# One ring for all row tiles, six tables with interleaved halves, new step times, and the reciprocal deviation by logarithm and exponential, in a two-layer graph kernel

## The chip, the cores and the metric

The kernel runs on one core of one Trainium2 chip. The metric is the device time of one execution in microseconds, the median of several runs. Engines are named as in the profile: PE (TensorE, matrix products), DVE (VectorE), ACT (ScalarE), POOL (GpSimd) and SP (SyncE, which here only issues transfers).

## What is computed

For each of 32 batches, x has 512 channels (C) and 1024 positions (N), in f32. The reference, cut to what matters:

```
h = relu(layernorm(x))                       # over the 1024 positions
q, k = wq . h, wk . h                        # one number per position
att = softmax(leaky(q[None, :] + k[:, None]))# 1024 x 1024, slope 0.01
x = x + relu(wm @ (h @ att.T) + bm)          # wm is the adjacency, 512 x 512
h = relu(layernorm(x))
x = x + W.T @ h + bias                       # W = adjacency * adjacency, by elements
```

The layer norm divides by sqrt(variance + 1e-5). The scores depend on a sum of two numbers only. So the kernel doesn't form the 1024 x 1024 matrix: it sorts the positions by q, makes running sums of the value rows in sorted order, weighted by exp(q) and exp(0.01 q), and picks for each position the two sums at the point where its own k changes the sign.

## The kernel before, in words

One batch goes through these steps. The names are functions of the kernel, the line numbers those of the profile.

- *load* (L400): four row tiles of 128 x 1024 f32 (512 KB) by SP's queue. *stats* (L414, L415, DVE): mean and variance. *norm* (L419, ACT): the square root of variance + eps. *slopes* (L423, L425, DVE): its reciprocal, and minus the mean times it. *relu* (L433, ACT): scales, shifts and clips the tile, in place in the first layer.
- *scores* (L445 PE, L450 ACT, L451): q and k as products; ACT copies them to SBUF, and a DMA writes them to a small DRAM row. *row* (L456) reads it back as a broadcast to 128 partitions, *columns* (L461, L466) turns it to columns.
- *rank* (L487, L492, L496, DVE): counts for each position how many q are smaller. *lower* (L503, ACT) counts by signs for k. *factors* (L473 to L480), *to_rows* (L523 to L529) and *from_rows* (L533 to L543) work out row numbers from the counts: `idx` for the scatter, `idg` for the gather.
- *value* (L550, PE, 64 products per batch) makes the value rows, *spread* (L557, ACT) copies them to SBUF, *scatter* (L562, L563, POOL, eight indirect DMAs) writes them in sorted order to a table `td` in DRAM, along with q as the last column. A row has 513 floats.
- *fetch* (L580, SP) reads the sorted rows back (2.36 MB) once all eight scatters have landed. *weights* (L587 to L592, ACT) and *later* (L600, L604, DVE) make the exponentials, *stationary* (L623, POOL) triangular masks times them, *totals* (L612, L613, L617) the sums of weights.
- *scan* (L636, L639, PE) makes running sums in nine steps. After each step, *sums* copies the last row into the next block of values as a carry (L648, L649, ACT), copies the sums to one of two tiles `t` (L651, L652, ACT), and SP writes those to the table (L654, L655). A next step waits for the carry.
- *gather* (L660, POOL, eight indirect DMAs) reads for each position one triple row: both sums and the value row between them. *excess*, *divide* (L669 to L681), *weigh* (L685, ACT) and *combine* (L689, DVE) put them together.
- *turn* (L696, PE transposes; L698, DVE) adds the result to x, which *reload* (L406, SP) has read anew. Then *stats*, *norm*, *slopes* and *relu* of the second layer follow, *lift* (L439, DVE) adds the bias, *propagate* (L703, PE, 64 products) and *finish* (L711, DVE) end the batch, and SP writes the tile out (L715).

Each table holds 1152 (9 x 128) triples of rows, two halves of 9 x 64. In a triple (k = 0, 1, 2) the first two places are the sums, which the scan writes, and the third is the value row that the scatter writes. In the table of before, the first half of the triples (o = 0) comes first and the second half (o = 1) after it; the scan's sums stand only in the first half. Five tables are used in turn (`TABLES`). The pads (L362 to L367) are rows that no position fills.

The work of all 32 batches is one list that is sorted by time (L719 to L769): a step of batch b stands at `b * T + PLAN[step]`, T is 80.647, with a shift for each of the first batches (FIRST, 5 batches) and of the last ones (LAST). These times only set an order: each engine executes its instructions in it, one after another, and each queue issues so too. Semaphores then see to dependences. The order is not altered by anything else (`manual_schedule`).

SBUF holds seven row tiles in a pool `xp`, seven in `yp` and four in `hp`. A new tile takes the oldest slot of its pool and waits until its last reader is done.

Of the kernel before, what the change touches and what calls it, by code (L numbers as in the profile page):

```python
# [9 lines left out]
F32 = mybir.dt.float32  # L10
BF16 = mybir.dt.bfloat16
U32 = mybir.dt.uint32
AF = mybir.ActivationFunctionType
ALU = mybir.AluOpType
# [11 lines left out]
TABLES = 5  # L26
PLAN = {
    "adjacency": (-108.2,),
    "biases": (103.637,),
    "columns": (-0.644,),  # L30
    "combine": (
        295.175, 296.981, 297.681, 298.56, 293.456, 294.898, 296.312, 299.441, 298.758,
        299.991, 297.356, 298.478, 299.289, 299.451, 296.18, 297.782,
    ),
    "compare_mask": (-39.924,),
    "divide": (279.776,),
    "excess": (274.084,),
    "factors": (31.052,),
    "fetch": (71.51,),
    "finish": (356.071, 361.635, 372.571, 377.123, 391.802, 417.732, 398.837, 420.531),  # L40
    "from_rows": (87.236,),
    "gather": (260.35, 264.453, 263.071, 264.447, 267.501, 263.458, 263.983, 262.344),
    "later": (82.669,),
    "lift": (343.707, 352.288, 361.264, 350.629),
    "load0": (-132.547,),
    "load1": (-83.561,),
    "load2": (-110.642,),
    "load3": (-58.45,),
    "lower": (25.135, 20.956, 15.44, 19.087, 14.733, 13.756, 46.166, 37.237),
    "masks": (-18.987,),  # L50
    "norm0": (-31.509,),
    "norm1": (326.35,),
    "pads": (-73.925,),
    "propagate": (346.423, 349.207, 352.169, 365.765, 371.233, 382.761, 381.981, 389.706),
    "rank": (17.984, 18.872, 20.129, 19.992, 25.594, 25.16, 26.367, 26.318),
    "reload0": (283.236,),
    "reload1": (289.947,),
    "reload2": (275.592,),
    "reload3": (294.126,),
    "relu0": (-21.389, -21.25, -20.652, -20.617),  # L60
    "relu1": (336.308, 336.463, 336.836, 338.53),
    "row": (1.149,),
    "scan": (88.672, 94.082, 102.974, 119.344, 135.342, 151.67, 171.394, 183.726, 197.836),
    "scatter": (49.236, 49.927, 49.759, 49.383, 53.226, 50.436, 50.301, 52.611),
    "scores": (-2.312,),
    "slopes0": (-23.106,),
    "slopes1": (327.104,),
    "spread": (10.418, 15.798, 4.081, 13.981, 26.765, 25.953, 18.654, 18.733),
    "square": (58.25,),
    "stationary": (82.87, 113.617, 158.362),  # L70
    "stats0": (-66.042, -57.278, -62.987, -37.25),
    "stats1": (317.836, 318.803, 321.449, 320.562),
    "sums": (90.354, 96.928, 115.433, 127.043, 139.894, 157.148, 175.982, 190.223, 211.407),
    "to_rows": (21.507, 28.041),
    "totals": (87.7,),
    "turn0": (305.575, 305.673, 305.631, 305.894),
    "turn1": (311.888, 311.406, 311.889, 311.693),
    "turn_adjacency": (-56.308,),
    "value": (4.654, 14.383, -2.141, 4.319, 19.868, 19.769, 15.801, 17.456),
    "weigh": (288.834, 288.645, 287.955, 288.582, 291.515, 291.657, 292.795, 290.433),  # L80
    "weights": (79.137,),
}
FIRST = {
    "columns": ((-42.337, 0), (-5.231, 0), (-2.394, 0), (1.4, 0), (-0.267, 0)),
    "combine": (
        (1.654, -0.5293), (1.005, -0.3379), (12.151, -0.5389), (4.662, 1.8664), (-2.717, -0.8902),
    ),
    "divide": ((-6.522, 0), (2.121, 0), (-5.673, 0), (4.125, 0), (-1.132, 0)),
    "excess": ((-1.018, 0), (2.997, 0), (-2.579, 0), (2.459, 0), (2.332, 0)),
    "factors": ((12.008, 0), (36.085, 0), (20.556, 0), (-17.001, 0), (38.59, 0)),  # L90
    "fetch": ((-13.827, 0), (-9.161, 0), (-4.562, 0), (-10.853, 0), (-1.955, 0)),
    "finish": (
        (-7.71, -0.5057), (2.749, -0.1853), (2.024, 0.1345), (-9.528, -0.7581), (-1.467, 0.1212),
    ),
    "from_rows": ((-16.545, 0), (143.901, 0), (-18.52, 0), (2.567, 0), (44.362, 0)),
    "gather": (
        (-9.577, -0.9485), (-11.32, -0.6577), (-4.449, 0.1722), (-9.629, -0.1251), (0.796, 0.0714),
    ),
    "later": ((-7.518, 0), (-7.347, 0), (-5.042, 0), (-3.972, 0), (4.883, 0)),
    "lift": (  # L100
        (18.493, -0.0414), (7.449, -0.8273), (15.021, 1.1896), (12.507, -0.3341), (13.391, 1.5716),
    ),
    "load0": ((-55.083, 0), (-28.454, 0), (-82.787, 0), (-89.755, 0), (-8.172, 0)),
    "load1": ((-101.05, 0), (-75.105, 0), (-63.613, 0), (-51.655, 0), (-0.85, 0)),
    "load2": ((-75.638, 0), (-49.315, 0), (-74.213, 0), (-72.717, 0), (-4.898, 0)),
    "load3": ((-124.613, 0), (-99.018, 0), (-53.784, 0), (-32.124, 0), (2.903, 0)),
    "lower": (
        (-42.973, -0.9302), (-15.708, -0.6946), (-9.312, -0.2971), (10.582, -0.0696), (34.856, -0.2988),
    ),
    "norm0": ((-83.601, 0), (-72.105, 0), (-7.68, 0), (-14.053, 0), (-0.379, 0)),  # L110
    "norm1": ((7.168, 0), (3.555, 0), (4, 0), (0.017, 0), (-5.5, 0)),
    "propagate": (
        (2.872, -0.6898), (4.018, -0.2375), (-1.06, -0.345), (-1.214, -0.2813), (-1.309, -0.0657),
    ),
    "rank": (
        (-28.589, 0.7379), (-2.87, -0.0721), (-9.055, 1.3394), (2.403, 0.1874), (-13.459, 0.0458),
    ),
    "reload0": ((-6.546, 0), (6.572, 0), (3.271, 0), (5.826, 0), (-6.189, 0)),
    "reload1": ((-1.43, 0), (8.813, 0), (6.594, 0), (3.913, 0), (-1.301, 0)),
    "reload2": ((-12.374, 0), (4.019, 0), (-0.514, 0), (8.006, 0), (-11.757, 0)),  # L120
    "reload3": ((1.756, 0), (10.208, 0), (8.663, 0), (2.721, 0), (1.743, 0)),
    "relu0": (
        (-45.821, -0.4234), (-30.012, 0.2683), (5.354, 1.299), (-1.745, 0.0153), (3.565, -0.5324),
    ),
    "relu1": (
        (9.188, 0.8499), (2.193, -0.013), (10.49, -0.8921), (-4.148, -0.0533), (5.006, -0.1977),
    ),
    "row": ((-24.758, 0), (-11.86, 0), (-11.402, 0), (-3.047, 0), (-12.236, 0)),
    "scan": (
        (-10.549, -0.0092), (-6.067, 0.0274), (-9.758, -0.1074), (-3.442, 0.0619), (-0.102, -0.002),  # L130
    ),
    "scatter": (
        (-17.315, 0.2618), (-11.153, 0.1679), (0.523, -0.1955), (-0.018, 0.156), (10.696, 0.3981),
    ),
    "scores": ((-62.327, 0), (-16.533, 0), (-8.214, 0), (-8.615, 0), (-9.042, 0)),
    "slopes0": ((-60.963, 0), (-35.582, 0), (0.527, 0), (-21.398, 0), (0.491, 0)),
    "slopes1": ((7.724, 0), (5.221, 0), (19.376, 0), (1.394, 0), (7.329, 0)),
    "spread": (
        (-20.028, 0.1376), (-6.015, 0.992), (8.718, 0.232), (10.947, -0.0528), (-1.297, 0.1468),
    ),  # L140
    "stationary": (
        (-9.533, -0.0517), (-0.489, 0.0893), (-5.756, -0.1735), (-6.449, -0.1248), (4.497, -0.0251),
    ),
    "stats0": (
        (-104.674, 0.702), (-77.356, 0.023), (-31.203, 0.8527), (-27.97, 0.4148), (-4.885, 0.5116),
    ),
    "stats1": (
        (1.142, 1.1308), (0.139, -0.1099), (5.326, 1.0258), (1.699, -0.7252), (-0.894, -0.2163),
    ),
    "sums": (  # L150
        (-8.312, -0.031), (-5.309, 0.0498), (-7.225, -0.0992), (-0.666, 0.0426), (1.428, -0.0107),
    ),
    "to_rows": (
        (-22.19, 0.5865), (-4.005, -0.1384), (-1.537, -0.1666), (6.658, -0.9288), (6.396, -0.6681),
    ),
    "totals": ((-8.637, 0), (-5.524, 0), (-8.905, 0), (-5.244, 0), (1.382, 0)),
    "turn0": ((-0.966, 0.9178), (2.05, 1.1944), (5.507, -0.2416), (13.541, 1.3559), (6.422, 0.711)),
    "turn1": (
        (-5.235, 2.5311), (3.046, 0.3048), (6.19, 0.6659), (-2.074, -0.6081), (-2.371, 1.8837),
    ),  # L160
    "value": (
        (-38.477, -0.2052), (-18.574, 0.6364), (-1.298, 0.5607), (-3.097, 0.6813), (-5.339, -0.0078),
    ),
    "weigh": (
        (-11.307, 0.6182), (-3.966, -0.0933), (3.637, 0.3643), (2.741, 0.6417), (-2.168, 0.2103),
    ),
    "weights": ((-7.839, 0), (-5.68, 0), (-3.274, 0), (-1.31, 0), (1.823, 0)),
}
LAST = {
    "columns": ((7.408, 0), (2.218, 0), (11.624, 0), (6.617, 0), (9.298, 0)),  # L170
    "combine": (
        (184.23, -0.647), (7.018, -0.6426), (4.54, 0.7582), (4.732, 1.7176), (6.572, -0.8403),
    ),
    "divide": ((175.719, 0), (2.439, 0), (-3.673, 0), (2.742, 0), (4.328, 0)),
    "excess": ((172.709, 0), (3.234, 0), (1.536, 0), (-5.245, 0), (8.713, 0)),
    "factors": ((-5.036, 0), (-12.606, 0), (17.188, 0), (-12.641, 0), (7.562, 0)),
    "fetch": ((5.667, 0), (1.995, 0), (5.156, 0), (-1.217, 0), (1.341, 0)),
    "finish": (
        (752.974, -0.831), (173.796, 0.1634), (35.432, 0.5906), (9.597, -0.1536), (9.066, 0.2434),
    ),  # L180
# [616 lines left out]
```

## Time and profile before

| | us |
|---|---|
| runs | 2375.03, 2374.95, 2371.89 (median 2374.95) |
| profiled execution, span | 2372.9 |
| PE busy | 2295.2 |
| DVE busy | 1952.6 |
| ACT busy | 1599.8 |
| POOL busy | 720.7 |

The profile's span runs from the first instruction to the last of the one profiled execution, for which no other time is given; two of the three runs are about 2 us over the span, one is 1 us below it. Lines of the profile name a kernel line, an engine and the tile that is written and read (`vs<-td` is the fetch, `td<-t` a write of sums, `g<-td,idg` a gather). A group shows its busy time, the mean of one instruction, and the idle time of the engine ahead of it with what ended that. In the page, DMA queue q1 holds the transfers that SP issues, q0 POOL's, q10 ACT's; the share is that of all 16 DMA engines of the core over the span. A window gives for a stretch of the span the busy time of each engine, the clock that was granted to PE, the DMA engines' share and the rate. The chain of waits follows the work back from what ended last, at each step to what released it. The names turn[0], totals[2] and the like mean a step of that batch.

### The profile page before, as it was taken

Reading aid. Unit: us, or ns where it says so; the run is one execution under the profiler, and the core shown is the slowest. Engines: PE = TensorE matmul, PEld = TensorE weight load, DVE = VectorE, ACT = ScalarE, POOL = GpSimd, SP = SyncE. Lnnn points to the kernel's source line nnn. Section 1 sums busy time; section 2 is a strip of 40 time slices with the busy share of each in tenths; the row PEclk is TensorE's granted clock in tenths of the full one; section 3 lists DMA queues with packets and bytes.
Section 4 is the critical chain, followed back from the end, with each engine's and each line's share of the span. In section 5 each row is a group of like instructions: output and inputs, shape, how many; then the busy total and the mean of one; then the engine's idle time right before and its main releaser. Section 6 shows DMA issues by size and latency. Waiting matters only on the chain.

```text
span 2372.9 us, 28069 instructions
## 1 busy us (share of the span) xinstructions
PE 2295.2 (97%) x7568; PEld 1011.5 (43%) x7568; DVE 1952.6 (82%) x5008; ACT 1599.8 (67%) x2880; POOL 720.7 (30%) x973
## 2 busy tenths in 40 slices
PE   7787999999999999999999999999999999999997
PEld 3233444444444444444444444444444444443443
DVE  7457888888888888888888888888888888888875
ACT  4576776766777766777676777676677676677551
POOL 2233333233333233233223233323333323233310
PEclk9988999999999999999999999999999999999998
DMA  6678888989999998999999999899988898998972
GB/s 222 171 181 277 284 284 277 296 269 276 287 290 285 296 286 266 277 299 283 288 292 266 276 294 287 287 291 272 268 291 276 288 302 253 276 282 269 311 294 79
DMA packets 206894, 643.45 MB, mean 271 GB/s; under 512 B 29120, under 2 KB 29248, under 8 KB 206736
## 3 DMA queue, kind: packets, MB, share of 16 engines
q1 hardware_dynamic: 142944, 355.74, 53.9%
q0 software_dynamic: 57344, 268.99, 30.7%
q10 hardware_dynamic: 6448, 16.92, 2.3%
q8 instruction: 61, 1.00, 0.2%
q14 instruction: 97, 0.79, 0.1%
HBM read 429.94 MB, written 211.60 MB: 270 GB/s over the span
## 4 chain that ended last, share of the span: by engine, by line
PE 85%; DMA 5%; DVE 5%; ACT 2%; issue 1%; POOL 1%; SPq 0%; ACTq 0%; another core or an unknown queue 0%; POOLq 0%; DVEq 0%
PE pg L703 34%; PE pv L550 33%; PE sc L639 10%; PE tr L696 4%; DMA vs<-td 2%; PE pq L445 2%; PE sc L636 1%; DVE g L689 1%; DVE st L414 1%; DMA g<-td,idg 1%; DMA td<-v,idx 1%; DVE junk L492 1%; ACT x L433 0%; DVE junk L487 0%; DMA x<-in_x_dram 0%
## 5 line engine op out<-in xcount | busy, mean ns | idle before, releaser
L703 PE MATMUL pg<-h,wsq 128*128 128x512 f32 x2048 | 911.2, 598 | 12.8 <-ACT h L433 12.8
L550 PE MATMUL pv<-wmT,x 128*128 128x512 f32 x2048 | 908.8, 598 | 5.9 <-ACT x L433 4.4
L703 PEld LDWEIGHTS pg<-h,wsq 128*128 128x128 f32 x2048 | 382.8, 191 | 517.4 <-issue 476.1
L550 PEld LDWEIGHTS pv<-wmT,x 128*128 128x128 f32 x2048 | 382.0, 191 | 499.1 <-issue 452.6
L623 POOL TENSOR_TENSOR sm<-mask_a,wc 128x192 f32<-128x192 f32 x96 | 51.9, 540 | 1254.9 <-DVE wc L600 785.7
L689 DVE SCALAR_TENSOR_TENSOR g<-g,cf 128x512 f32<-128x512 f32 x512 | 357.9, 756 | 46.4 <-ACT g L685 44.3
L648 ACT COPY vs<-sc 1x512 f32<-1x512 f32 x256 | 145.3, 567 | 272.9 <-PE sc L639 208.6
L563 POOL DMA_INDIRECT td<-v,idx x256 | 272.4, 1064 | 149.3 <-POOL v L562 36.3
L639 PE MATMUL sc<-vs,sm 128*64 128x512 f32 x1024 | 282.6, 621 | 21.3 <-POOL sm L623 11.1
L503 ACT ACTIVATE junk<-qrow,qk 128x1024 bf16<-128x1024 f32 x256 | 294.0, 1148 | 5.5 <-DMA qrow<-qd 2.5
L660 POOL DMA_INDIRECT g<-td,idg x256 | 243.5, 951 | 147.4 <-issue 71.5
L698 DVE SCALAR_TENSOR_TENSOR y<-tr,nbm,y 128x512 f32<-128x512 f32 x256 | 174.4, 744 | 66.3 <-PE tr L696 61.2
L711 DVE SCALAR_TENSOR_TENSOR y<-pg,bm_sb,y 128x512 f32<-128x512 f32 x256 | 185.8, 731 | 32.4 <-PE pg L703 32.0
L651 ACT COPY t<-sc 128x512 f32<-128x512 f32 x288 | 168.0, 583 | 40.7 <-DMA td<-t 35.3
L433 ACT ACTIVATE x<-x,nmr,rstd 128x1024 f32<-128x1024 f32 x128 | 148.6, 1231 | 64.9 <-DVE nmr L425 64.9
L492 DVE TENSOR_SCALAR_CACHE_REDUCE junk<-qrow,qk,cnt 128x896 bf16<-128x896 f32 (+6 forms) x224 | 180.5, 806 | 8.2
L685 ACT ACTIVATE g<-g,cf 128x512 f32<-128x512 f32 x256 | 167.7, 712 | 6.4 <-DVE cf L679 5.3
L487 DVE TENSOR_SCALAR_CACHE_REDUCE junk<-qrow,qk 128x128 bf16<-128x128 f32 (+6 forms) x224 | 166.0, 741 | 6.6
L414 DVE BATCH_NORM_STATS2 st<-x 128x6 f32<-128x512 f32 x256 | 162.7, 677 | 9.6 <-DMA x<-in_x_dram 9.6
L439 DVE TENSOR_TENSOR y<-y,bias_sb 128x1024 f32<-128x1024 f32 x128 | 154.3, 1219 | 16.0 <-ACT h L433 16.0
L557 ACT COPY v<-pv 128x512 f32<-128x512 f32 x256 | 141.8, 579 | 29.7 <-PE pv L550 14.0
L414 DVE BATCH_NORM_STATS2 st<-y 128x6 f32<-128x512 f32 x256 | 160.4, 668 | 0.0
(111 smaller groups left out, 1923.1 us busy)
## 6 DMA issues: line engine op xcount, KB each, us to landing
vs<-td SPq DMA_DIRECT2D x192, 384.8 KB
td<-t SPq DMA_DIRECT2D x576, 128.2 KB
x<-in_x_dram SPq DMA_DIRECT2D x128, 512.0 KB
y<-in_x_dram SPq DMA_DIRECT2D x128, 512.0 KB
out_dram<-y SPq DMA_DIRECT2D x128, 512.0 KB
qrow<-qd ACTq DMA_DIRECT2D x32, 512.0 KB
td<-v,idx POOLq DMA_INDIRECT x256, 8.3
g<-td,idg POOLq DMA_INDIRECT x256, 13.8
```

The costliest lines, as they stand in the source:

```text
L414: nc.vector.bn_stats(st[:, i, :], s.x[c][:, ts(i, HALF)])
L492: nc.vector.tensor_scalar(junk[:, j * P :], s.qrow[:, j * P :], qc, first, ALU.is_lt, ALU.add, accum_out=s.cnt[:, 1, j : j + 1],)
L503: nc.scalar.activation(junk, s.qrow, AF.Sign, bias=s.qk[:, 1, j : j + 1], accum_out=s.sgn[:, j : j + 1])
L550: nc.tensor.matmul(pv, s.h[c][:, ts(j, P)], wmT[:, c, :], start=(c == 0), stop=(c == NC - 1))
L563: i = nc.gpsimd.indirect_dma_start(tds[s.b % TABLES][:, :], bass.IndirectOffsetOnAxis(ap=s.idx[j // 4][:, j % 4 : j % 4 + 1], axis=0), v[: ...
L639: nc.tensor.matmul(p[ts(k, HP), :], m[:, k, :], s.vs[h][:, 0:C], start=True, stop=True)
L651: nc.scalar.copy(t[:, 0:C], p)
L660: nc.gpsimd.indirect_dma_start(s.g[:, j, :], None, tds[s.b % TABLES][0 : 3 * NB * HP, :].rearrange("(s k) w -> s (k w)", k=3), bass.Indire ...
L689: nc.vector.scalar_tensor_tensor(r, s.g[:, j, k * W : k * W + C], s.cf[:, k, j : j + 1], r, ALU.mult, ALU.add)
L698: nc.vector.scalar_tensor_tensor(xh, pt, nbm[:, o : o + 1], xh, ALU.max, ALU.add)
L703: nc.tensor.matmul(pg, wsq[:, r, ts(c, P)], s.h[r][:, ts(i, HALF)], start=(r == 0), stop=(r == NC - 1),)
L711: nc.vector.scalar_tensor_tensor(xh, s.pg.pop((c, i)), bm_sb[:, c : c + 1], xh, ALU.add, ALU.add)
```

## The change

1. *One ring.* The pools `xp`, `yp` and `hp` become one pool of 18 tiles.
2. *New times.* PLAN, FIRST and LAST have new numbers, with six batches in FIRST and LAST; T stays. *pads* and *holes* have a time per table.
3. *Tables.* Six in place of five, and four DRAM rows for q and k in place of two. The halves of a table are interleaved in blocks of 64, so that the sorted rows lie on 128 partitions in one transfer: three fetch DMAs per batch in place of six. Row numbers are worked out to match, with one small DVE operation more. A gather's source is now the whole table.
4. *Pads.* A pad tile per table, with its own memsets; three DMAs per table.
5. *Holes.* The places k = 0, 1 of the second halves are written by no step. A new step fills them once per table, with the first 9 x 64 x 1026 numbers of x (2.36 MB), by one DMA of SP's queue from DRAM to DRAM.
6. *Reciprocal deviation.* ACT makes exp(-0.5 ln(variance + eps)) and DVE improves it by one Newton step. The set of ACT tables is loaded once ahead of all.

The diff, without the numbers of the plan. `-`/`+` lines stand in the order of the code.

```diff
-TABLES = 5
+TABLES = 6
+ROWS = 18
+QROWS = 4
 PLAN = {
-    "adjacency": (-108.2,),
+    "adjacency": (-1664.69,),
...
-    "pads": (-73.925,),
+    "holes": (-0.276, 48.82, 31.32, 105.504, 154.636, 169.546),
+    "pads": (-50.462, -29.172, -74.596, -76.152, -71.484, -110.523),
...
-    xp = ctx.enter_context(tc.tile_pool(name="xp", bufs=7))
-    yp = ctx.enter_context(tc.tile_pool(name="yp", bufs=7))
-    hp = ctx.enter_context(tc.tile_pool(name="hp", bufs=NC))
+    xp = ctx.enter_context(tc.tile_pool(name="xp", bufs=ROWS))
...
-        rows = td.rearrange("(o h s k) w -> o s h k w", o=2, s=HP, k=3)
-        return rows[:, :, h : h + n, 2, :]
+        rows = td.rearrange("(h p k) w -> p h k w", p=P, k=3)
+        return rows[:, h : h + n, 2, :]
...
-    root = const.tile([P, 1], F32, name="root")
-    nc.scalar.activation(root, eps_sb, AF.Sqrt)
+    nc.scalar.preload_act_table_set("natural_log_exp_and_others")
...
-    def pads(s):
-        pad = vp.tile([P, W], F32, tag="v", name="pad")
+    def pads(s, i):
+        pad = vp.tile([P, W], F32, tag="v", name=f"pad_{i}")
         nc.vector.memset(pad, 0.0)
         nc.vector.memset(pad[:, C : C + 1], FAR)
-        for td in tds:
-            for o in range(2):
-                nc.sync.dma_start(sorted_rows(td, 0, NB - 1)[o, 0], pad[0 : NB - 1, :])
-                nc.sync.dma_start(sorted_rows(td, NB - 1, 1)[o, :, 0], pad[0:HP, :])
+        for o in range(2):
+            nc.sync.dma_start(sorted_rows(tds[i], 0, NB - 1)[o * HP], pad[0 : NB - 1, :])
+        nc.sync.dma_start(sorted_rows(tds[i], NB - 1, 1)[:, 0], pad)
+
+    def holes(s, i):
+        rows = tds[i].rearrange("(h o s k) w -> h o s (k w)", o=2, s=HP, k=3)[:, 1, :, 0 : 2 * W]
+        flat = x.rearrange("b c n -> (b c n)")[0 : NB * HP * 2 * W]
+        nc.sync.dma_start(rows, flat.rearrange("(h s w) -> h s w", h=NB, s=HP))
...
     def norm(s, layer):
         s.std = sp.tile([P, NC], F32, tag=f"std{layer}", name=f"std{layer}_{s.b}")
-        nc.scalar.activation(s.std, s.mv[:, :, 1], AF.Sqrt, bias=eps_sb)
+        nc.scalar.activation(s.std, s.mv[:, :, 1], AF.Ln, bias=eps_sb)
+        s.rstd = sp.tile([P, NC], F32, tag=f"rstd{layer}", name=f"rstd{layer}_{s.b}")
+        nc.scalar.activation(s.rstd, s.std, AF.Exp, scale=-0.5)
 
     def slopes(s, layer):
-        s.rstd = sp.tile([P, NC], F32, tag=f"rstd{layer}", name=f"rstd{layer}_{s.b}")
-        nc.vector.reciprocal(s.rstd, s.std)
+        t = sp.tile([P, NC], F32, tag=f"step{layer}", name=f"step{layer}_{s.b}")
+        nc.vector.scalar_tensor_tensor(t, s.mv[:, :, 1], EPS, s.rstd, ALU.add, ALU.mult)
+        nc.vector.scalar_tensor_tensor(t, t, -0.5, s.rstd, ALU.mult, ALU.mult)
+        nc.vector.scalar_tensor_tensor(s.rstd, t, 1.5, s.rstd, ALU.add, ALU.mult)
...
-        odd = 3.0 * NB * HP
+        odd = 3.0 * HP
...
-        nc.vector.scalar_tensor_tensor(s.idx[i], block, 3.0, rk, ALU.mult, ALU.add)
+        nc.vector.scalar_tensor_tensor(
+            s.idx[i], block, 3.0 * (P - PAIRS), rk, ALU.mult, ALU.add
+        )
...
-        nc.vector.scalar_tensor_tensor(s.idg, pair, 1.0, block, ALU.add, ALU.add)
+        nc.vector.tensor_scalar(block, block, float(P - PAIRS), 1.0, ALU.mult, ALU.add)
+        nc.vector.tensor_tensor(s.idg, pair, block, ALU.add)
...
-            for o in range(2):
-                d = nc.sync.dma_start(t[ts(o, HP)], sorted_rows(tds[s.b % TABLES], 3 * i, 3)[o])
-                for k in s.sc:
-                    tc.add_manual_dep(d.ins, k.name, DONE, reason="any of them may hold a row")
+            d = nc.sync.dma_start(t, sorted_rows(tds[s.b % TABLES], 3 * i, 3))
+            for k in s.sc:
+                tc.add_manual_dep(d.ins, k.name, DONE, reason="any of them may hold a row")
...
-        nc.sync.dma_start(td[ts(ha, HP), 0, :], t[0:HP, :])
-        nc.sync.dma_start(td[ts(hb, HP), 1, :], t[HP:P, :])
+        nc.sync.dma_start(td[ts(2 * ha, HP), 0, :], t[0:HP, :])
+        nc.sync.dma_start(td[ts(2 * hb, HP), 1, :], t[HP:P, :])
...
-            tds[s.b % TABLES][0 : 3 * NB * HP, :].rearrange("(s k) w -> s (k w)", k=3),
+            tds[s.b % TABLES].rearrange("(s k) w -> s (k w)", k=3),
```

The instructions that the change puts in another order in the ramp, as the compiled order has them: SP issues the adjacency first of all, then eleven row tiles; the pads of tables 0 and 1 come after their memsets, which stand on DVE between the rank pieces of batch 0; then the holes of table 0; after fetch[0] the holes of tables 2 and 1, and later, between the writes of sums of batches 0 and 1, those of tables 3, 4 and 5.

## The prediction

> **What bounds the kernel now.** I read the busy times and the DMA queues of the page first, then the windows by stage, then what TensorE (PE) waited for, then the chain of waits of the first 240 us.
>
> ```profile
> PE 2295.2 (97%) x7568; PEld 1011.5 (43%) x7568; DVE 1952.6 (82%) x5008; ACT 1599.8 (67%) x2880; POOL 720.7 (30%) x973
> ...
> q1 hardware_dynamic: 142944, 355.74, 53.9%
> q0 software_dynamic: 57344, 268.99, 30.7%
> ```
>
> ```profile
> 0.00:240.00 240.00, 187.36 (x628) 77.85 (x628) 143.45 (x454) 146.82 (x278) 66.88 (x107) 0.93 0.74 211
> 240.00:2100.00 1860.00, 1859.18 (x6195) 823.57 (x6196) 1606.51 (x4126) 1324.69 (x2379) 594.89 (x789) 1.00 0.91 284
> 2100.00:2373.00 273.00, 248.62 (x746) 110.08 (x744) 202.62 (x430) 128.30 (x225) 58.92 (x77) 0.95 0.72 238
> ```
>
> The columns of the windows are length, PE, PEld, DVE, ACT, POOL, granted clock, DMA share, GB/s. From 240 to 2100 us PE is busy for 1859.18 of 1860 us: that stage is PE's own work, which the change leaves alone. Idle are 52.6 us in the first 240 us (the ramp) and 24.4 in the last 273 (the tail). Only there can the change gain, though it can lose anywhere. The ramp's idle time is made by transfers:
>
> ```profile
> 67.55 0.06 ACT w L589
> ...
> 68.94 0.57 POOL sm L623
> 69.52 0.04 issue
> 69.56 1.72 PE sc L639 x4
> ...
> 96.79 7.00 DMA td<-v,idx
> 103.93 0.62 SPq L580
> ...
> 107.26 9.96 DMA vs<-td
> ...
> 118.01 0.52 POOL sm L623
> ...
> 146.16 6.35 DMA td<-t
> ...
> 171.35 1.01 POOL g L660
> ...
> 180.13 16.16 DMA g<-td,idg
> ```
>
> This is the chain (start, length, what). Batch 1's scatter lands at 103.8, its sorted rows are fetched from 103.93 to 117.3, and only then come its masks (118.01) and totals. Batch 0's gathers start at 171.35 and end at 196.3; the first transposes of batch 0 (turn[0], L696) start at 214.15. PE executes in a written order, so what comes late here is late at the end, unless other work stands in front of it.
>
> **Removed: table loads.** ACT has 61+28+27+6+1 = 123 table loads of 1.283 us, 157.8 us; one stays. In the steady stage ACT is busy for 1324.7 of 1860 us and PE waits for nothing, so they are worth 0. In the ramp there are 8, one of them on the chain (93.64, ahead of the scatter): at most -1.3, and nothing if something later holds that scatter.
>
> **Added: Exp and Newton step.** Per normalisation one more ACT activation (about 0.30, as L419) and three DVE operations of 0.16 in place of a reciprocal of 0.17: +0.6 us of latency. 64 of them give 19 us of ACT and 20 us of DVE (82% to 83%), hidden under PE. Only the first and the last are on the path: +0.6 each.
>
> **Fetch and tables.** Three fetch DMAs of 128 partitions instead of six of 64 save SP three issues of 0.61, at most -1.8 per batch. The bytes stay (2.36 MB), so between -1.8 and 0; I take 0. A sixth table frees nothing that is waited for in the steady stage.
>
> **One ring.** 7+7+4 slots become 18. In both orders a slot is asked for after its last reader, with some PE work in between in every case, so I cost it at 0. The cover is PE's queue of work in order; if it were gone, each late tile would cost about one landing, 4 to 6 us (x from 166.18 took 4.20, the first one 5.74).
>
> **New times.** In PE's written order, counted with the durations of the rows, the work ahead of totals[0] to [2] grows by 6.7, 2.2 and 1.5 us, that ahead of turn[0] shrinks by 1.1. So alone they move the ramp by about -1 to +2. In the tail the last chain (ACT h before the last pg, 10.3 us of wait) gets 0.6 longer and up to 5 us more work is laid beside it: -2 to +1, I take 0.
>
> **Added: holes.** Six DMAs from DRAM to DRAM on SP's queue copy 2.36 MB each, 14.2 MB in the ramp. By the compiled order scatter[b] waits for holes[b], and the gathers too. No row of before is such a copy. Bounds for one: 6.4 us, if all 16 engines work at q0's rate (268.99 MB in 30.7% of 16 x 2372.9 us = 23.1 GB/s per engine); 15.7 us, if it gets no more than q1's mean over the span (355.74 MB / 2372.9 us = 150 GB/s). Added bytes on the queue gain nothing. The nearest row has the same bytes on the same queue: the fetch, 103.93 to 117.31, 13.4 us from issue to landing; less some 2 us for three issues, I take **11.4 us**, 13.4 to landing.
>
> The same table holds the case for and against. At 240 us x 0.26 = 62 us the engines are free long enough for six holes of 6.4 to 8.5 us (8.5 is q1's 17.4 GB/s per engine on all 16), but not where they stand.
> - fetch[0]: the holes of table 0 are queued in SP behind pads that need a DVE memset, and that memset stands behind four rank pieces (1.7 + 3 x 2.05 us), the maximum (1.8) and another memset (0.5 each). The adjacency, loaded first, delays x by 1.05 MB / 308 GB/s = 3.4, Newton by 0.6: ranks start at 29 instead of 25.0. So the memset ends at about 40, SP has five more issues, the holes go out at 43 and land at 56.4. Eight scatters at 1.5 us and a landing of 5 follow: fetch[0] at 73.5, before 52.8: **+20.7**. With holes for nothing it would be 64.5, since the second index tile is ready at about 53 (+ 4 scatters at 1.5, + 5).
> - fetch[1]: holes 2 and 1 follow fetch[0] on the queue, and scatter[1] waits for both: 73.5 + 3 x 11.4 + 2 = 109.7, then 12 + 5: 126.7, before 103.9: +22.8. Masks and totals[1] follow at 141.4, before 118.6.
> - Behind the holes 3 to 5 in SP's queue stand the writes td<-t of batches 0 and 1; they free the two t tiles, for which ACT waits (already 35.3 us over the run), and ACT's carry rows, for which PE waits, stand behind it.
> - turn[0]: at the least totals[1] at 141.4, 35.8 us of PE work to totals[2] and 24.7 to turn[0], plus the 15.5 us that PE waited between totals[1] and [2] before (118.6 to 170.7, less 36.6 of work): 217.4, **+3.3**. At the most batch 0's own chain moves as one by fetch[0]'s delay: 234.9, **+20.7**. Neither end has a row that is nearer; the middle is **+12**.
>
> DMA: Bandwidth & Descriptors of the Trainium skill (section "Why a DMA increments its semaphore by 16 and not by 1", on how many engines) speaks against this copy. It says that a transfer is cut over the largest number up to 16 that divides the slowest dimension of both sides. Here these are 9 and 576, so 9 engines, an estimate of 11.4 us at 23.1 GB/s or 15.1 at 17.4; no row of before shows such a shape. By it the sum would be 2387 to 2397, while an even spread would be the first rival's.
>
> **Sum.** Ramp +12, steady 0, tail 0, start and end inside those. The profiled span is 2372.9; of the three runs one lies under it (2371.89), and the median, 2374.95, is 2 us over it. 2372.9 + 12 = 2385, with those 2 us **2387**.
>
> **Rivals.**
> 1. *The copies are cheap and the new order pays: faster.* At 6.4 us the holes are no longer what scatter[1] waits for (64.5 + 3 x 6.4 + 2 = 85.7, and its values come at 82.6 to 97.8 in before), so batches 1 and 2 stay on time: totals[2] at 171, 24.7 us of work, turn[0] at 196 to 200 instead of 214.15, where before PE waited 16 us (43.4 less 27.2 of work) for gathers that stood behind the masks of batch 2 on POOL. -14: **2361**. For it: the 62 us of free DMA time. Against it: batch 0 is later by 11.7 even so. Between -14 at 6.4 us and +12 at 11.4 the sign changes at about 9 us a hole: below that it decides. Chance 0.28.
> 2. *Nothing measurable:* between the two prices delay and reordering cancel, **2375**, chance 0.12.
> 3. *The new order opens gaps in the steady stage:* DMA at 0.91 and DVE at 86% leave little room; one wait of 0.8 us per batch over 26 batches adds 21: with half the ramp's loss **2402**. Against it: in before nothing waits with the same slots and T. Chance 0.07.
> 4. *The change doesn't do what it says:* loads might stay if the tables don't share one set; ACT would then keep its 67%, worth 0 either way, so this moves nothing and has no chance of its own.
>
> **How the numbers follow.** The forecast has 0.53. The prices 6.4 and 15.7 bound the ramp: -14 at the one, and about +30 at the other (fetch[1] +40, of which about 10 are covered as above). The range is 2358 to 2405; it leaves out about 0.2. About 0.2%, 4.75 us, can be told from no change. Faster 0.28; same 0.13 (the second rival and the forecast's lower end); slower 0.59.
>
> **What would show it.** Right: PE's busy time from 240 to 2100 still full; more than 60 us of PE idle in the first 250; fetch[0] at 70 to 77 and fetch[1] after 120; scatters that wait for the holes' landing; ACT t waiting for td<-t in the ramp. Wrong: holes that land within 9 us of issue, fetch[1] at about 104 and turn[0] before 205 (first rival); idle PE in the middle (third). One table load left and ACT near 61% show the reciprocal deviation's part; if the time fell with the ramp unchanged, ACT was on the path after all and my zero for the loads is wrong. A tail whose last wait is far from 10.3 us would void the zero there.

## The result, and the profile after

The changed kernel takes 2477.03 us (median of four runs, 2471.21 to 2486.75), the kernel before 2374.99 (four runs): a ratio of 1.0432, 95% interval 1.0406 to 1.0459. So it is slower by about 102 us, where I had forecast slower by 12 with a range up to 2405. The profiled execution (span 2484.9) is the longest of the four.

The page of the changed kernel: busy times and DMA queues.

```profile
span 2484.9 us, 28067 instructions
...
PE 2316.7 (93%) x7568; PEld 1018.6 (41%) x7568; DVE 1983.4 (80%) x5178; ACT 1436.7 (58%) x2821; POOL 700.5 (28%) x973
...
q1 hardware_dynamic: 145014, 370.21, 47.3%
q0 software_dynamic: 57344, 268.99, 28.4%
```

The windows of the changed kernel (length, PE, PEld, DVE, ACT, POOL, granted clock, DMA share, GB/s):

```profile
0.00:240.00 240.00, 148.36 (x457) 62.28 (x458) 108.11 (x369) 96.75 (x190) 48.37 (x83) 0.80 0.75 233
240.00:2100.00 1860.00, 1821.65 (x6059) 800.14 (x6059) 1591.58 (x4164) 1158.25 (x2287) 558.40 (x773) 0.99 0.80 274
2100.00:2485.00 385.00, 346.69 (x1054) 156.19 (x1052) 283.68 (x646) 181.69 (x345) 93.70 (x118) 0.96 0.69 241
```

PE executes the same 7568 products. It is idle for 168.2 us (2484.9 - 2316.7) in place of 77.7, that is 90.5 more, and busy for 21.5 us more, as the clock that it is granted is lower in the stages where it stands still more (0.80 in place of 0.93 in the first 240 us). Together that is the whole difference of the two spans, 112 us. From 600 to 1800 us PE is as full as before, where it was busy for all 1200:

```profile
600.00:1800.00 1200.00, 1198.25 (x4022) 529.11 (x4021) 1057.62 (x2746) 758.82 (x1502) 366.76 (x510) 1.00 0.83 283
```

The chain of waits of the changed kernel's first 330 us (start, length, what), to be held against the chain in the prediction:

```profile
46.33 17.53 DMA td<-in_x_dram
...
81.19 0.38 SPq L773
...
98.71 20.79 DMA td<-t
...
129.97 15.95 DMA td<-v,idx
146.09 0.39 SPq L773
...
179.87 20.51 DMA td<-t
...
211.94 0.38 SPq L773
212.42 0.43 SPq L773
212.94 23.01 DMA vs<-td
```

The first *holes* DMA takes 17.53 us from issue to landing. fetch[0] is issued at 81.2 (before 52.8), fetch[1] at 146.1 (103.9), fetch[2] at 211.9 (155.6). A write of sums behind the holes takes 20 us to land in place of 6. Batch 1's first scatter stands 23 us on POOL for the holes (view: what POOL waited for, from 90 to 135 us):

```profile
POOL td L757 <- DMA td<-in_x_dram: 23.0, 1, 23.0
```

All that was foreseen in kind. But it isn't the whole loss, as the experiments show. They are read by three stages: the start of batch 9's score products (L445, L636 after) from the timeline of PE, from there to batch 27's, and from there to the end. The stages are of the one profiled execution; the ratio is of all runs against the runs of the kernel before on the same chip. So where the two differ, the ratio counts: several chips were used, on which the kernel before itself takes from 2366.5 to 2377.7 us, and the profiled execution lies up to 10 us from its kernel's median. The score products are also not at quite the same place of PE's list: with the new times 1711 products stand ahead of batch 9's (e2), with the old ones 1734 (e5), most of the difference short transposes, about 4 us by an estimate from their durations.

| kernel | ratio (95%) | to batch 9 | 9 to 27 | 27 to end |
|---|---|---|---|---|
| before | 1 | 579.7 | 1269.5 | 523.7 |
| after | 1.0432 (1.0406-1.0459) | 660.8 | 1268.2 | 555.9 |
| e1 holes cut along 64 rows | 1.0397 (1.0368-1.0426) | 639.8 | 1267.8 | 563.1 |
| e2 old tables, no holes | 1.0448 (1.0430-1.0467) | 644.3 | 1270.4 | 573.7 |
| e3 before + new reciprocal deviation | 1.0017 (1.0008-1.0026) | 578.9 | 1269.5 | 524.3 |
| e4 holes on ACT's queue | 1.0513 (1.0491-1.0536) | 668.5 | 1267.7 | 559.1 |
| e5 as e2, old times | 0.9999 (0.9988-1.0009) | 582.6 | 1269.5 | 522.3 |
| e6 as e2, gathers moved | 1.0321 (1.0304-1.0338) | 617.5 | 1270.7 | 560.2 |
| e7 as after, gathers moved | 1.0432 (1.0395-1.0469) | 647.2 | 1267.7 | 553.2 |
| e8 as e1, gathers moved | 1.0357 (1.0340-1.0375) | 642.3 | 1267.6 | 554.3 |
| e9 as e2, old times to batch 9 | 1.0224 (1.0207-1.0242) | 581.2 | 1276.4 | 573.5 |
| e10 as e2, old times from batch 22 | 1.0372 (1.0353-1.0391) | 637.8 | 1295.5 | 521.4 |
| e11 as e2, new times for 10 to 21 only | 1.0142 (1.0125-1.0159) | 584.1 | 1303.6 | 526.1 |
| e12 as e6, ranks of 3 to 7 earlier | 1.0329 (1.0308-1.0350) | 627.1 | 1271.5 | 557.4 |
| e13 as after, old times | 1.0115 (1.0098-1.0131) | 603.5 | 1269.4 | 519.4 |
| e14 as e1, old times | 1.0102 (1.0083-1.0121) | 602.8 | 1269.4 | 519.3 |
| e15 as e6, early start as before | 1.0307 (1.0289-1.0324) | 616.5 | 1270.5 | 553.2 |
| e16 as e2, old times for 0 to 3 | 1.0368 (1.0351-1.0385) | 605.7 | 1271.3 | 565.6 |

The changed kernel loses 81 us to batch 9 and 32 after batch 27.

### The profile page after: what moved, and what is told of

Its sections match the earlier page's. It is cut to its first block, busy times and chain, and to the rows that moved or that the text cites. A ratio compares the mean times of both kernels' runs of the same rounds, so it can differ in the third digit from the quotient of the medians.

```text
span 2484.9 us, 28067 instructions
## 1 busy us (share of the span) xinstructions
PE 2316.7 (93%) x7568; PEld 1018.6 (41%) x7568; DVE 1983.4 (80%) x5178; ACT 1436.7 (58%) x2821; POOL 700.5 (28%) x973
## 4 chain that ended last, share of the span: by engine, by line
PE 76%; DMA 13%; DVE 5%; ACT 3%; issue 1%; POOL 1%; SPq 0%; ACTq 0%; POOLq 0%; DVEq 0%
PE pg L896 32%; PE pv L744 28%; PE sc L832 8%; DMA vs<-td 5%; PE tr L889 4%; DMA td<-t 3%; PE pq L636 2%; DMA td<-v,idx 2%; PE sc L829 1%; DVE st L602 1%; DVE junk L683 1%; DMA td<-in_x_dram 1%; POOL td L757 1%; DMA x<-in_x_dram 1%; DMA out_dram<-y 1%
## 5 line engine op out<-in xcount | busy, mean ns | idle before, releaser
L744 PE MATMUL pv<-wmT,x 128*128 128x512 f32 x2048 | 928.5, 606 | 12.2 <-ACT t L844 8.3
L896 PEld LDWEIGHTS pg<-h,wsq 128*128 128x128 f32 x2048 | 386.8, 191 | 519.3 <-issue 470.5
L757 POOL DMA_INDIRECT td<-v,idx x256 | 284.4, 1111 | 331.6 <-ACT cf L864 104.7
L683 DVE TENSOR_SCALAR_CACHE_REDUCE junk<-qrow,qk,cnt 128x768 bf16<-128x768 f32 (+6 forms) x224 | 180.5, 806 | 8.2
L678 DVE TENSOR_SCALAR_CACHE_REDUCE junk<-qrow,qk 128x256 bf16<-128x256 f32 (+6 forms) x224 | 164.6, 735 | 10.9 <-DMA qrow<-qd 6.1
L878 ACT ACTIVATE g<-g,cf 128x512 f32<-128x512 f32 x256 | 160.9, 714 | 5.2 <-DVE cf L872 5.2
L624 ACT ACTIVATE h<-y,nmr,rstd 128x1024 f32<-128x1024 f32 x128 | 149.1, 1231 | 7.5 <-DMA out_dram<-y 3.7
```

The source lines that it names most:

```text
L683: nc.vector.tensor_scalar(junk[:, j * P :], s.qrow[:, j * P :], qc, first, ALU.is_lt, ALU.add, accum_out=s.cnt[:, 1, j : j + 1],)
L744: nc.tensor.matmul(pv, s.h[c][:, ts(j, P)], wmT[:, c, :], start=(c == 0), stop=(c == NC - 1))
L757: i = nc.gpsimd.indirect_dma_start(tds[s.b % TABLES][:, :], bass.IndirectOffsetOnAxis(ap=s.idx[j // 4][:, j % 4 : j % 4 + 1], axis=0), v[: ...
L896: nc.tensor.matmul(pg, wsq[:, r, ts(c, P)], s.h[r][:, ts(i, HALF)], start=(r == 0), stop=(r == NC - 1),)
```

## The experiments

**Holes, times or parts: the first four.** My theory after the result was that the holes are dearer than I had priced them, by the engines that they use (A) or by bytes and place in the queue (B). The rival was that the new times lose by themselves (C).

e1:

```diff
-        nc.sync.dma_start(rows, flat.rearrange("(h s w) -> h s w", h=NB, s=HP))
+        nc.sync.dma_start(
+            rows.rearrange("h s w -> s h w"), flat.rearrange("(s h w) -> s h w", h=NB, s=HP)
+        )
```

> The holes copied with the 64 rows as the slowest dimension in place of the 9 blocks; same bytes, same places, same order of instructions. Theory A (the holes take too long one by one: 17.5 us from issue to landing for the first, because they use only part of the engines): each lands in 8 to 11 us, fetch[1] comes at 110 to 120 in place of 146, and the time falls by 40 to 80 us, to 2395 to 2435. Theory B (the bytes are what costs, or the place in SP's queue): landing stays at 15 us or more and the time stays above 2455. Theory C (the new times are worse by themselves): the holes land sooner, but the time falls by less than 25.

Two windows of the changed kernel, and two of e1, in which the first holes are under way:

```profile
52.00:56.00 4.00, 2.01 (x33) 0.94 (x32) 3.79 (x12) 0.83 (x2) 0.00 (x0) 1.00 0.55 212
60.00:63.00 3.00, 3.00 (x7) 1.40 (x6) 2.93 (x9) 0.00 (x0) 0.00 (x0) 0.77 0.57 230
```

```profile
50.00:54.00 4.00, 3.93 (x37) 1.51 (x35) 3.68 (x16) 1.63 (x4) 0.00 (x0) 1.00 1.02 274
54.00:57.00 3.00, 1.29 (x5) 0.82 (x6) 2.72 (x13) 0.37 (x1) 0.00 (x0) 1.00 1.03 343
```

The mean DMA share (the column before the last) is 0.55 and 0.57 with 9 as the slowest dimension (0.63 in the four us between) and 1.02 and 1.03 with 64. In the four us before these windows, with tiles of x under way too, it is 0.86 and 0.79. With 9 it stays near half, with 64 it is full, and the first holes land in 12.9 us in place of 17.5. 9 of 16 is 0.56, so the rule of the Trainium skill's page DMA: Bandwidth & Descriptors (section "Why a DMA increments its semaphore by 16 and not by 1") that the prediction weighed agrees with this case. But only some 8 us of 102 go, and the two intervals overlap: the engines' share is not the main cause.

e2 takes the layout of before (halves one after another, six fetches, gathers from the first half) into the changed kernel, and drops the holes, which that layout doesn't need:

```diff
-        rows = td.rearrange("(h p k) w -> p h k w", p=P, k=3)
-        return rows[:, h : h + n, 2, :]
+        rows = td.rearrange("(o h s k) w -> o s h k w", o=2, s=HP, k=3)
+        return rows[:, :, h : h + n, 2, :]
...
-            plan(s, holes, "holes")
```

> The changed kernel with the table layout of before (halves one after another, six fetch DMAs of 64 partitions, gathers from the first half), so without holes; new times, one ring, six tables and the new reciprocal deviation stay. Theory A and B (holes): the whole loss goes, 2350 to 2390. Theory C (new times or the ring): 2440 or more stays.

The ratio is 1.0448: without any holes nothing is won, against my theory. The stages say why this can mislead: it is 16 us better to batch 9, and 18 worse after batch 27. In these two profiles two effects cancel, and neither is the bulk; by the ratios the two kernels can't be told apart.

e3 puts only the new *norm* and *slopes* and the one table load into the kernel before.

> The kernel before with nothing but the new reciprocal deviation (logarithm, exponential, Newton step; 123 table loads become 1). My forecast for this part: no change, 2370 to 2380, PE busy from 240 to 2100 as full as before, ACT busy lower by about 140. Rival: ACT's waits in the ramp and tail shorten and 3 to 10 us are gained.

ACT is busy for 1453.0 us in place of 1599.8, one table load is left, and from 240 to 2100 us PE is as full as before, within 2.2 us:

```profile
240.00:2100.00 1860.00, 1857.01 (x6188) 822.05 (x6186) 1623.63 (x4219) 1196.04 (x2318) 595.72 (x787) 1.00 0.90 283
```

The time is 0.17% above before, the stages are equal within 1 us. So 147 us less of ACT's work gain nothing: ACT is not what PE waits for.

e4 issues the holes by `nc.scalar.dma_start`.

> The changed kernel with the holes issued by ACT's queue in place of SP's. If the loss comes from what stands behind the holes in SP's queue (writes of sums, tiles), those now pass the holes: 2395 to 2440, and the waits of ACT for td<-t shrink from 50 us in the first 600. If it comes from the scatters that wait for the holes, or from the engines that the holes keep busy, the time stays within 20 us of 2477.

The ratio is 1.0513 (two runs): 19 us more. The writes of sums are held less (ACT's waits for td<-t fall from 50.3 to 33.2 us in the first 600), but ACT's own broadcast of the scores now stands behind the holes (38.4 us of ACT's waits for it in place of 17.0). The other queue moves the wait and doesn't remove it.

**The times, and gathers that collide.** e5 gives e2 the step times of the kernel before (PLAN, FIRST, LAST; all six pads at -73.925).

> The second experiment's kernel (one ring, six tables of the old layout, no holes, new reciprocal deviation) with the step times of the kernel before put back. Theory C (the new times are what costs): 2370 to 2385. Rival (the ring of 18 or the sixth table costs): 2440 or more.

0.9999: ring, sixth table, four score rows and reciprocal deviation cost and gain nothing. e2 differs from it in the step times alone, so they make the 106 us of e2.

Where? In e2 around 324 us fetch[4] and seven of the eight gathers of batch 2 start together. The timeline of SP, then of POOL, of e2 (start, length, engine, line, operation, out<-in; in brackets the idle time ahead and what ended it), and the transfer in its chain of waits:

```profile
324.48 5.29 SPq L771 DMA_DIRECT2D vs<-td  x6
```

```profile
324.79 1.00 POOL L851 DMA_INDIRECT g<-td,idg  x1 [1.85 <-PE tr L887]
...
332.33 0.94 POOL L851 DMA_INDIRECT g<-td,idg  x1 [0.30 <-issue]
356.56 0.51 POOL L814 TENSOR_TENSOR sm<-mask_a,wc 128x192 f32<-128x192 f32 x1 [23.29 <-DVE wc L791]
357.02 0.51 POOL L814 TENSOR_TENSOR sm<-mask_b,wc 128x192 f32<-128x192 f32 x1
357.68 0.98 POOL L851 DMA_INDIRECT g<-td,idg  x1
```

```profile
329.02 26.74 DMA vs<-td
```

The masks that PE needs come 32 us after their fetch was issued, in before's steady stage 17.7. PE is busy for 19.77 of the 37 us from 320 to 357. In before the gathers of batch b stand behind the first masks of batch b+2 on POOL's list (but for batches 28 and 29), so they cannot start until that fetch has landed:

```profile
921.84 11.82 SPq L580 DMA_DIRECT2D vs<-td  x6
```

```profile
939.50 0.51 POOL L623 TENSOR_TENSOR sm<-mask_a,wc 128x192 f32<-128x192 f32 x1 [26.16 <-DVE wc L600]
939.96 0.51 POOL L623 TENSOR_TENSOR sm<-mask_b,wc 128x192 f32<-128x192 f32 x1
940.62 1.01 POOL L660 DMA_INDIRECT g<-td,idg  x1 [0.15 <-issue]
```

In the new times all or most of them stand ahead of those masks for batches 0 to 3 and 27 to 29. e6 puts them behind:

```diff
+    masks_at = {a[0].b: t for t, _, f, a in steps if f is stationary and a[1] == 0}
+    for n, (t, k, f, a) in enumerate(steps):
+        if f is gather and a[0].b + 2 < B:
+            steps[n] = (max(t, masks_at[a[0].b + 2] + 0.2), k, f, a)
     steps.sort(key=lambda e: e[:2])
```

> The second experiment's kernel, with one thing changed in its times: no gather of batch b stands ahead of the first masks of batch b+2 on POOL's list (it does for batches 0 to 3 and 27 to 29, up to 40 units of plan time; in the kernel before only for 28 and 29, by 6 and 10). Theory D (a gather of 6.3 MB that is issued while the fetch of batch b+2 is under way makes that fetch take 22 to 32 us in place of 14 to 18, and PE waits for its masks): fetch to masks falls below 20 us for batches 2 to 5, and the time falls by 50 to 100 us, to 2380 to 2430. Rival E (the fetches are late because of other things in the new times, such as the scatters that stand later, and the collision is only a sign of it): less than 25 us are gained.

In e6 the same fetch has its masks after 14.3 us, and the gathers follow:

```profile
308.43 4.14 SPq L771 DMA_DIRECT2D vs<-td  x6
```

```profile
322.77 0.51 POOL L814 TENSOR_TENSOR sm<-mask_a,wc 128x192 f32<-128x192 f32 x1 [16.31 <-DVE wc L791]
323.24 0.51 POOL L814 TENSOR_TENSOR sm<-mask_b,wc 128x192 f32<-128x192 f32 x1
323.89 1.01 POOL L851 DMA_INDIRECT g<-td,idg  x1 [0.15 <-issue]
```

```profile
311.94 9.97 DMA vs<-td
```

The ratio falls from 1.0448 to 1.0321, about 30 us (the medians differ by 28). In the two profiled executions it is 27 in the head and 13.5 after batch 27; e2's was 9 us above its median and e6's 3 below. The collision is real and dear, but it is little more than a quarter of e2's loss, and little more than half of the least that I expected (50).

e7 makes the same move in the whole changed kernel.

> The same move of the gathers in the whole changed kernel, with its holes. Theory D: 40 to 90 us gained, 2390 to 2435; the holes then hold what is left. Rival E: less than 25 gained.

No gain in the ratio, where I had expected 40 to 90 us. So in the changed kernel itself the gathers' place explains nothing that can be measured: with the holes something else is late where the collisions were. That it is the holes themselves, e8 suggests.

e8 is e7 with the holes of e1.

> The same move, with the holes cut along their 64 rows as in the first experiment. If holes and collisions add up, it is 5 to 20 us faster than the kernel with the moved gathers alone; if the holes matter only while the gathers collide, the same within 5.

1.0357, some 18 us below e7; below e1 by 9, with intervals that just overlap. So the better cut seems to be worth more once the gathers are moved.

**Head and tail.** e9, e10 and e11 take e2 and choose the times by batch, with `s.b < 10`, `s.b >= 22` and `not 10 <= s.b < 22` for the old ones:

```diff
-        times = PLAN[name]
+        use = (OLD_PLAN, OLD_FIRST, OLD_LAST) if s.b < 10 else (PLAN, FIRST, LAST)
+        times = use[0][name]
```

> The second experiment's kernel (old tables, no holes), with the step times of the kernel before for batches 0 to 9 and the new times for the rest. By the starts of the score products, that kernel loses 65 us to batch 9 and 50 us after batch 27. Theory G (two separate losses, one by the new times of the first batches, one by those of the last): 2415 to 2435, batch 9 at 580 to 590. Rival (the tail is bad because the head left the pipeline in another state): 2370 to 2390, both losses gone.

> The same kernel with the new times up to batch 21 and the times of before from batch 22. Theory G: the head's 65 us stay, the tail's 50 go, 2425 to 2450. Rival: the tail's loss stays, 2475 or more.

> The same kernel with the new times only for batches 10 to 21. The period there is 70.20 us with the new times and 70.52 with those of before, in all runs so far. Theory G: 2368 to 2376, that is 0 to 6 us below the kernel before. Rival (the shorter period is paid back at the seams): 2376 or more.

e9 reaches batch 9 at 581.2 and still takes 573.5 after batch 27, to the microsecond e2's 573.7; e10 still has 637.8 and then 521.4. So head and tail lose for themselves: the tail's loss is no echo of the head's. The cut itself costs 6 us where old times go over to new ones and 25 the other way (9 to 27: 1276.4 and 1295.5, e2 1270.4), which I hadn't counted. Hence e11, made to beat both kernels, doesn't: with new times in the middle the period is 70.20 us per batch in place of 70.52, some 4 us in 12 batches, and both cuts cost 34 (1303.6 against 1269.5). No kernel here is faster than before.

**What else in the times.** e12 takes 12 units off the times of scores, row, columns, factors, ranks, lower, to_rows and from_rows of batches 3 to 7 in e6.

> The kernel of old tables with the moved gathers, and the scores, the row, ranks and row numbers of batches 3 to 7 earlier by 12 units of plan time. Theory F (in the new times the ranks of batch b+4 stand on DVE between the landing of gather b and the scatter of batch b+4, which makes the round of gather, row numbers, scatter, fetch and masks 80 us long in place of 70.5, from batch 1 to 5): the round falls below 76, 10 to 30 us are gained, 2420 to 2443. Rival (something else sets the round): within 8 us of 2453.

1.0329 against 1.0321: nothing is gained. From gather[1] to gather[2] it is 80.6 us as in e6 (80.1; in e5 71.9), and batch 4's score products start at 238 us in place of 241: so something else holds them. Theory F falls in this form. Whether loads, norms and relu that come earlier too would help was not tried.

e15 puts three early steps of e6 where before has them:

```diff
+    soon = {adjacency: -300.0, turn_adjacency: -80.0, pads: -70.0}
+    for n, (t, k, f, a) in enumerate(steps):
+        if f in soon:
+            steps[n] = (soon[f], k, f, a)
```

> The kernel of old tables, new times and moved gathers, with three more steps put where the kernel before has them: the adjacency after the first batch's tiles, its transposes after the first score products, all pads before the ranks of batch 0. Theory H (the late start of batch 0, 13 us at its first row numbers and 16 at fetch[0], goes through to the end): 12 to 18 us less than 2453. Rival (it is covered later, since batches 2 and 3 are only 7 us late): within 6 of 2453.

1.0307 against 1.0321, the intervals overlap (the medians differ by 13 us, but the kernel before is 11 us quicker on this chip). The move did little, though: fetch[0] is issued at 65.5 us, in e6 at 68.6, in before at 52.8. So the late start was hardly taken away, and this run can't show what it costs. In e6 fetch[0] is 16 us later than in before and fetch[2] only 7. The next run says more.

e16 is e9 with `s.b < 4`.

> The second experiment's kernel with the times of before for batches 0 to 3 alone. If the head's loss of 65 us is made by the times of the first four batches: 2415 to 2440, as with ten. If it is made by those of batches 4 to 9, which come late for their scores and ranks (score products of batch 4 at 241 to 247 us in place of 219): 2460 or more.

1.0368, between the two: of e2's 106 us some 19 go, of the 53 that ten batches bring. The first fetches come when e9's do (fetch[0] at 54.3 and 53.7, fetch[2] at 153.9 and 156.5), and no gather of the head stands ahead of the masks. Yet fetch[4] is late by 18 us, in e16 first, then in e9:

```profile
308.43 2.61 SPq L997 DMA_DIRECT2D vs<-td  x4
```

```profile
290.30 2.61 SPq L997 DMA_DIRECT2D vs<-td  x4
```

So neither a late start nor the gathers' place is needed for the loss from batch 4 on, of which the step over from old to new times may be a part.

**The forecast's own question.** e13 is the whole changed kernel with the times of before, with the holes at the changed kernel's six times; e14 the same with the holes of e1.

> The whole changed kernel (ring, six tables with interleaved halves, holes at the same six times, new reciprocal deviation) with the step times of the kernel before. My forecast's theory, that the holes are dear in the ramp: +12 or more, 2385 to 2410, with the fetches of batches 0 and 1 late. Rival (the other half of the ramp's slack hides them): 2372 to 2380.

> The same with the holes cut along their 64 rows. If the share of the engines that one hole gets is what costs: half of the loss of the run before goes. If the bytes cost: the same within 4.

e13: 1.0115, 27 us above before. e5 differs from it only in layout and holes, so with the old times these two cost 27 us together. By the stages 21 of it fall before batch 9 (603.5 against 582.6), while the end is 3 us shorter (519.4 against 522.3); the two ran on different chips. The changed kernel differs from e13 in the step times alone: 1.0432 against 1.0115, so beside the holes the new times cost 75 us. e14 is 1.0102: the better cut gains nothing that can be told. The windows of e13:

```profile
0.00:240.00 240.00, 166.05 (x518) 66.17 (x518) 126.27 (x431) 123.48 (x244) 58.25 (x97) 0.86 0.74 243
240.00:2100.00 1860.00, 1857.39 (x6247) 825.20 (x6248) 1627.93 (x4244) 1190.80 (x2319) 601.01 (x792) 1.00 0.85 283
2100.00:2392.00 292.00, 270.45 (x804) 118.92 (x803) 228.81 (x505) 137.10 (x260) 64.70 (x85) 0.97 0.71 251
```

PE's idle time in the first 240 us is 74 us, before 52.6, and from 240 to 2100 us it is full within 3 us: this is the loss that the prediction had described.

## Why the prediction was wrong

- **What bounds the kernel:** right, but the stages were drawn too narrow. PE stays full from 600 to 1800 us, within 3 us, in the changed kernel, e2, e5, e6, e13 and e14, and their losses lie in head and tail. The sign that I had named, a full PE from 240 to 2100 us, did not come: it is idle there for 38 us (1860 - 1821.65), since the head's loss goes on past 240 us and the tail's begins before 2100.
- **Table loads, Exp and Newton step, one ring:** right, 0 (e3, e5). Only one load is left and ACT is at 58%.
- **Holes:** right in kind, too low in size. I took 13.4 us to landing, it was 17.5, from 46.3 and not from 43; fetch[0] came at 81.2 and not 73.5, fetch[1] at 146.1 and not 126.7. With the old times holes and layout cost 27 us (e13), where the ramp's term said +12, between +3.3 and +20.7. The +30 that I kept for the dearest holes is near it, but it would have reached only 2405.
- **New times: the step that failed.** The prediction has "So alone they move the ramp by about -1 to +2", and for the tail "-2 to +1, I take 0". Measured, they cost 75 us beside the holes (the changed kernel against e13) and 106 without them (e2 against e5; in the profiles 62 to batch 9 and 51 after batch 27). I had counted PE's list and taken its depth as the measure. But in the ramp work goes round over several lists: gather, row numbers, scatter, fetch, masks, gather. I looked at POOL's list only to price the first rival, and there read gathers that no longer stand behind masks as a part of its gain of 14 us. Without the holes the runs show the reverse: such gathers are under way together with the fetch that PE waits for (32 us to its masks in place of 14), and putting them back gains about 30 us (e6).
- **Tail:** its 0 rested on one wait of 10.3 us. That wait hardly changed (12.2), but 32 us were lost after batch 27 all the same. So a last wait that stays the same does not show that the tail does, as I had supposed.
- **The steady stage's rival:** it didn't come. The new times have even the shorter period there, 70.20 us against 70.52.

Of the 102 us, then, holes and layout cost 27 with the old times, and the new times bring the other 75. That the new times are the bulk is shown; it isn't a sum of fixed parts, since e2 without holes is no faster. Why they cost so much is shown only in part. Without holes, about 30 of 106 us are the gathers' place; with the holes as they are, moving the gathers gains nothing (e7). What makes the other 76 of e2 (38 to batch 9 and 36.5 after batch 27 in e6, against before) stays open. The ranks of batches 3 to 7 are not it (e12), and the late start is not needed for the loss from batch 4 on (e16). In e6 the round from gather[1] to gather[2] is 80 us in place of 72, and every list has other neighbours.

## What to carry to other kernels

When a written order is replaced, the depth of the bounding engine's list says little, as it did here: go through the lists of all queues, and ask of every large transfer what it can now be under way with. A wait that seems idle (gathers behind masks) can be what keeps two transfers apart. An experiment that takes out two parts at once can show zero where two effects cancel, so read it by stages before concluding.

## What the runs showed of the hardware

- A copy in DRAM of 9 x 64 rows has a DMA share of 0.55 and 0.57 in two windows (0.63 between them), one of 64 x 9 rows 1.02 and 1.03. The first of them lands in 17.5 and 12.9 us, both above the 6.4 of my lower bound.
- Seven gathers of 5.5 MB (7 x 788 KB) beside a fetch of 2.36 MB: the masks come 32 us after the issue (e2), without them 14 (e6).
- Where PE stood still more, its granted clock was lower too. From 90 to 150 us it is busy for 33.5 us in the changed kernel, with a clock of 0.73, and for 47.1 in before, with 0.94. Over the run the same products took 21.5 us more, so the loss was larger than the idle time, 112 against 90.5 us. The rows of the changed kernel, then of before:

```profile
90.00:120.00 30.00, 15.48 (x72) 6.39 (x72) 17.90 (x57) 12.99 (x27) 5.95 (x7) 0.73 0.67 202
120.00:150.00 30.00, 18.03 (x35) 6.78 (x36) 8.53 (x25) 13.00 (x28) 9.94 (x17) 0.73 0.84 203
```

```profile
90.00:150.00 60.00, 47.05 (x146) 17.49 (x144) 32.18 (x114) 43.56 (x86) 17.89 (x31) 0.94 0.68 175
```

- Issuing can take long: in e13, with three holes one after another, SP needed up to 10.8 us to issue one of them, and 15.9 for the tile behind them.

```profile
32.66 12.33 SPq L371 DMA_DIRECT2D td<-in_x_dram  x2
45.03 15.94 SPq L403 DMA_DIRECT2D x<-in_x_dram  x1
```
